# Two residual additions of a four-layer graph network made by accumulating DMAs instead of VectorE

## The chip, the cores and the metric

The kernel runs on one core of a Trainium2 chip. The core has TensorE (PE, matrix products), VectorE (DVE), ScalarE (ACT), GpSimd (POOL) and SyncE (SP, which here only issues DMAs), each with an instruction queue of its own that is worked off in order, and 16 DMA engines that all queues share. The metric is the device time of one execution in microseconds; less is better.

## The reference

32 batches of 512 tokens with 128 features pass through four residual layers, all with one 512x512 adjacency matrix. Cut to what matters (`ln_relu` is the normalization of a token's features followed by max with 0):

```python
# layer 0: graph convolution
h = ln_relu(x);  x = x + (A_norm @ h) @ W.T + b0        # A_norm: normalized adj + I
# layer 1: five gated steps
h0 = h = ln_relu(x)
for _ in range(5):
    m = adj @ h                                          # used for both m_in and m_out
    u3 = h @ u3_w.T + u3_b
    z = sigmoid([m, m] @ w3_w.T + w3_b + u3)
    r = sigmoid([m, m] @ w4_w.T + w4_b + u3)
    hv = tanh([m, m] @ w5_w.T + w5_b + (r * h) @ u5_w.T + u5_b)
    h = (1 - z) * h + z * hv
x = x + h
# layers 2 and 3: attention over the edges of adj
x = x + elu(attention(ln_relu(x)));  x = x + attention(ln_relu(x))
```

The two additions that the change touches are the `+ b0` of layer 0 and the `x + h` at the end of layer 1.

## The kernel before, in words

Everything stays in fp32 in SBUF. A batch's x is one tile of 128 partitions by 4 token chunks by 128 features (256 KB, 2 KB in each partition). There are nine such tiles, and later four more in the memory of the transposed adjacency, which the profile calls "adjT".

Each batch goes through these stages:

- `gcn` (layer 0), for pairs of batches: `norm_relu` takes statistics on VectorE (L508, L512), computes factor and offset with four small GpSimd operations (L520, L521, L522, L525), and normalizes on ScalarE (L527). `in_three` multiplies by the adjacency in three rounded products (L644), with a rescaling by ScalarE (L626) in between. `out_mm` multiplies by W (L717). L704 adds b0 to x, and L725 adds the product. For the first four batches (`first`) L721 does the last step chunk by chunk.
- `ggnn` (layer 1): five times `step`, in six lanes, so that six batches are under way at once. The products are L644, L755 and L758, the gates are ScalarE's L788, L795, L799, and VectorE's L790 to L804 form the new state `new`, which has features on the partitions.
- After a step `shuttle` turns the state back to tokens on the partitions: VectorE transposes blocks of 32 by 32 into `sq` (L594), four DMAs write these to the DRAM tile `far` (L597), and one DMA reads it back into `h` (L599). After the last step L819 adds `h` to x. Steps that lie very early or late in the order go through TensorE instead (L586), and L812 adds; for the last step these are batches 28 to 31. `shuttle_first` (L604, L607, L610) does the same way back in the other direction before the first step.
- `gat` for layers 2 and 3: statistics and normalization as above, products L871, scores L914, mixing L940 (or L926 for the last batches), and the residual additions L955 to L973.

No loop issues these instructions directly. Every stage is handed as an `op` to a planner (`Plan`), with an engine, an assumed duration, a due time, the values it reads and writes, and a delay until its result is to be used. The planner simulates the engines in 16 attempts, chooses the attempt with the earliest end, and emits the instructions in that order. So each engine's order is fixed at build time, and durations and delays in the source decide it. Its prices on the lines concerned are 0.6 us for a large VectorE operation, 0.44 and 0.4 us for an SP issue, 1.2 us for each small GpSimd operation of a norm, and 4 and 5 us for a DMA's landing. An `op` with an empty function only marks an order. A `lane` is held by a batch from its first step to its last addition into x.

Of the kernel before, what the change touches and what calls it, by code (L numbers as in the profile page):

```python
# [14 lines left out]
ALU = mybir.AluOpType  # L15

P = 128
# [4 lines left out]
Q = P // W  # L22
# [248 lines left out]
def gnn_stack(ctx: ExitStack, tc: tile.TileContext, a: dict, out: bass.AP):  # L271
    nc = tc.nc
    x, adj = a["x"], a["adj"]
    B, N, D = x.shape
    C = N // P
# [9 lines left out]
    def flat(t):  # L285
        return t.rearrange("p c k -> p (c k)")
# [35 lines left out]
    op = plan.op  # L322
    MM, MM1, TURN, MR = 0.858, 0.224, 0.111, 0.2325
    V, A, COPY = 0.6, 0.575, 0.505
# [12 lines left out]
    def load(name, shape, src, due, kind=None, delay=4.7):  # L337
        v = Val(kind) if kind else fixed(shape, name)
        op("SP", 0.45, due, lambda: nc.sync.dma_start(matrix(v)[:, :shape[1]], src), w=[v], delay=delay)
        return v  # L340
# [20 lines left out]
    xs = []  # L361
# [6 lines left out]
    for c in range(C):  # L368
        e, q = (("ACT", nc.scalar), ("SP", nc.sync))[c % 2]
        op(e, 0.45, -1001, lambda c=c, q=q: q.dma_start(adj_sb.t[:, c, :], adj[c * P:(c + 1) * P, :]),  # L370
           w=[adj_sb[c]], delay=(3.2, 4.7, 4.4, 4.9)[c])
    w0 = load("w0", [P, D], a["L0_gnn_W"], -993.9, "m", delay=5.6)
    b0 = load("b0", [P, D], bass.AP(tensor=a["L0_gnn_b"].tensor, offset=a["L0_gnn_b"].offset,
                                    ap=[[0, P], [1, D]]), -993.4)

    op("DVE", 0.2, -38.7, lambda: nc.vector.tensor_scalar_add(b0.t, b0.t, -1.0), w=[b0])
    for k in ("w4", "w3", "w5", "u3", "u5"):
        src = a[f"L1_gnn_{k}_w"]
# [17 lines left out]
    for c in range(C):  # L396
        p = Val("bank")
# [16 lines left out]
    for m in range(C):  # L414
        op("DVE", 0.26, -800 + 0.7 * m, lambda m=m: nc.vector.tensor_add(diag.t[:, m, :], block(adjT.t, m), ident.t),
           r=[adjT, ident], w=[diag[m]])
# [69 lines left out]
    for k, u, half in (("w4", "u3", True), ("w3", "u3", True), ("w5", "u5", False)):  # L486
        gate_b[k] = fixed([P, 1], "gate_b" + k)
        op("DVE", 0.1, -14, lambda k=k, u=u: nc.vector.tensor_add(gate_b[k].t, raw["b" + k].t, raw["b" + u].t),
           r=[raw["b" + k], raw["b" + u]], w=[gate_b[k]])
# [4 lines left out]
    for i, l in enumerate((2, 3)):  # L494
        p = Val("bank")
        op("PE", 0.3, 9, lambda i=i, l=l, p=p: nc.tensor.matmul(p.t[:, 0, :2], gats.t[:, i, :], a_pair[l].t, start=True, stop=True),
           r=[gats, a_pair[l]], w=[p])
# [89 lines left out]
        op("PE", C * TURN, due, turns, r=[y, ident], w=[p, *then])  # L587
        return p

    def shuttle(src, squares, dst, due, soon):  # L590


        sq, far = Val("sq"), Val("far", Q)
        op("DVE", 0.626, soon, lambda: nc.vector.transpose(  # L594
            sq.t.rearrange("p q (c j) -> p q c j", c=C), flat(src.t).rearrange(squares, c=C, q=Q)), r=[src], w=[sq])
        for k in range(Q):
            op("SP", 0.44, due, lambda k=k: nc.sync.dma_start(  # L597
                far.t[:, :, k, :].rearrange("q i f -> i q f"), sq.t[k * W:(k + 1) * W]), r=[sq], w=[far[k]], delay=4)
        op("SP", 0.4, due, lambda: nc.sync.dma_start(dst.t, far.t.rearrange("q i k f -> (q i) k f")), r=[far], w=[dst], delay=5)  # L599

    def shuttle_first(h, hT, due, soon):
# [94 lines left out]
    def gcn(pair, due):  # L696
        first, ys = pair[0] < 4, []
        for i, b in enumerate(pair):
            y = Val("y", C)
            if b == 0:  # L700
                norm_first(b, y)
            else:
                norm_relu(b, y, -797 if b == 1 else due + i, dinv if first else None)
            op("DVE", V, due + i + 3.8, lambda b=b: nc.vector.tensor_add(  # L704
                xs[b].t, xs[b].t, b0.t[:, None, :].to_broadcast([P, C, D])), r=[b0], w=[xs[b]])
            ys.append(y)

        ms = [product(y, due + i) if first else in_three(y, False, factors["an"], due + i) for i, y in enumerate(ys)]
        if b == 1:
            factors["adj"] = factors_of(adjT, "adj", -3.6, ys[0])  # L710
            factors["an"] = normalized(ms[0])
        for i, (b, m) in enumerate(zip(pair, ms)):
            p = Val("bank")

            def out_mm(m=m, p=p):
                for c in range(C):
                    nc.tensor.matmul(p.t[:, c, :], m.t[:, c, :], w0T.t[:, 0, :], start=True, stop=True)  # L717
            op("PE", C * MM1, due + i + 3.3, out_mm, r=[m, w0T], w=[p])
            if first:
                for c in range(C):  # L720
                    op("DVE", 0.26, due + i - 0.5, lambda b=b, c=c, p=p: nc.vector.scalar_tensor_tensor(  # L721
                        xs[b].t[:, c, :], p.t[:, c, :], dinv.t[:, c:c + 1], xs[b].t[:, c, :], op0=ALU.mult, op1=ALU.add),
                       r=[p, dinv], w=[xs[b][c]])
            else:
                op("DVE", V, due + i + 1.5, lambda b=b, p=p: nc.vector.tensor_add(flat(xs[b].t), flat(xs[b].t), flat(p.t)),  # L725
                   r=[p], w=[xs[b]])
# [23 lines left out]
    def step(b, s, m, hT, due, lane):  # L750
        gate, r, rh, z, cand = Val("bank"), Val("r"), Val("rh"), Val("z"), Val("bank")
        split = isinstance(m, tuple)

        def weigh(p, i, moving, start=False, of=None):
            nc.tensor.matmul(flat(p.t), (of or gates).t[:, i, :], flat(moving.t), start=start, stop=True, skip_group_check=True)  # L755

        def one_pass(p, i, moving, start, of):
            nc.tensor.matmul(flat(p.t), of.t[:, i - 1, :], flat(moving.t), start=start, stop=True, skip_group_check=True)  # L758

        def by_m(p, i, at, start, *more):  # L760

            rest = [x for _, _, reads in more for x in reads]

            def others():
                for of, moving, _ in more:
                    weigh(p, 0, moving, of=of)
            if not split:
                def whole():
                    weigh(p, i, m, start)
                    others()  # L770
                op("PE", (1 + len(more)) * MM, at, whole, r=[m, gates, *rest], w=[p])
                return
            upper, lower, across = m
            upper_of, lower_of, across_of = of_gates

            def first_two():
                one_pass(p, i, upper, start, upper_of)
                one_pass(p, i, lower, False, lower_of)

            def third_one():  # L780
                one_pass(p, i, across, False, across_of)
                others()
            op("PE", 2 * MR, at, first_two, r=[upper, lower, upper_of, lower_of], w=[p])
            rescale(p, at - 5)
            op("PE", MR + len(more) * MM, at, third_one, r=[across, across_of, *rest], w=[p])

        by_m(gate, 1, due + 0.2, True, (gates, hT, [hT, gates]))
        op("ACT", A, due - 5, lambda: nc.scalar.activation(flat(r.t), flat(gate.t), AF.Tanh, bias=gate_b["w4"].t, scale=0.5),  # L788
           r=[gate, gate_b["w4"]], w=[r])
        op("DVE", V, due - 5, lambda: nc.vector.scalar_tensor_tensor(flat(rh.t), flat(r.t), 1.0, flat(hT.t), op0=ALU.add, op1=ALU.mult),  # L790
           r=[r, hT], w=[rh])
        if split:
            rescale(gate, due - 5, 1 / (1 + 1 / SPLIT))
        by_m(gate, 2, due + 0.3, False)
        op("ACT", A, due - 5, lambda: nc.scalar.activation(flat(z.t), flat(gate.t), AF.Tanh, bias=gate_b["w3"].t, scale=0.5),  # L795
           r=[gate, gate_b["w3"]], w=[z])
        hv, new = Val("hv"), Val("hT")
        by_m(cand, 3, due + 0.4, True, (u5T, rh, [rh, u5T]))
        op("ACT", A, due - 5, lambda: nc.scalar.activation(flat(hv.t), flat(cand.t), AF.Tanh, bias=gate_b["w5"].t),  # L799
           r=[cand, z, gate_b["w5"]], w=[hv])  # L800
        op("DVE", V, due - 5, lambda: nc.vector.tensor_sub(flat(hv.t), flat(hv.t), flat(hT.t)), r=[hT], w=[hv])  # L801
        op("DVE", V, due - 5, lambda: nc.vector.scalar_tensor_tensor(flat(hv.t), flat(z.t), 1.0, flat(hv.t), op0=ALU.add, op1=ALU.mult),
           r=[z], w=[hv])
        op("DVE", V, due - 5, lambda: nc.vector.scalar_tensor_tensor(flat(new.t), flat(hv.t), 0.5, flat(hT.t), op0=ALU.mult, op1=ALU.add),  # L804
           r=[hv, hT], w=[new])

        last = s == STEPS - 1
        h = Val("h", C)
        if not EARLY <= due < STEPS * B:
            p = to_features(new, due + 2, *([] if last else [h]))  # L810
            if last:
                op("DVE", V, due + 2, lambda: nc.vector.tensor_add(flat(xs[b].t), flat(xs[b].t), flat(p.t)),  # L812
                   r=[p, lane], w=[xs[b]])
            else:
                op("ACT", COPY, due + 1, lambda: nc.scalar.copy(flat(h.t), flat(p.t)), r=[p], w=[h])
            return h, False, new
        shuttle(new, "p (c q i) -> p q c i", h, due, due - 5)
        if last:
            op("DVE", V, due + 2, lambda: nc.vector.tensor_add(  # L819
                xs[b].t.rearrange("p c (k j) -> p k c j", k=Q), xs[b].t.rearrange("p c (k j) -> p k c j", k=Q),  # L820
                h.t.rearrange("p k (c j) -> p k c j", c=C)), r=[h, lane], w=[xs[b]])
        return h, True, new


# [210 lines left out]
```

## Time and profile before

| | before |
|---|---|
| median of 3 runs | 1515.34 us (1513.87 to 1516.15) |
| profiled execution | 1513.58 us, span 1511.7 us |
| PE busy | 1498.9 us (99%) |
| PE weight load busy | 1153.8 us (76%) |
| DVE busy | 1430.9 us (95%), 3431 instructions |
| ACT busy | 1236.2 us (82%) |
| POOL busy | 292.9 us (19%), 496 instructions |
| DMA of SP's queue | 155.66 MB, 39.6% of 16 engines' time |
| granted TensorE clock | 1.0 |

Busy time is the time in which at least one instruction of the engine is recorded. The records of VectorE's large operations overlap a little, so the spacing of their starts (0.60 us) is below a record's length (0.68 us). Ends of matmuls are modelled. The times of a row's instructions are means over one execution.

### The profile page before, as it was taken

To read this page: it belongs to the slowest core of one execution; us is meant where nothing else is said; L and a number is where in the kernel's file an instruction comes from. 1 tells how busy PE (TensorE), PEld (TensorE's weight loads), DVE (VectorE), ACT (ScalarE), POOL (GpSimd) and SP (SyncE) were. 2 spreads that over 40 slices of the span, in tenths; PEclk is the share of its full clock that TensorE was granted. 3 is DMA by queue.
4 is the path that set the end of the run, shared out by engine and by line. 5 is a ranking of instruction groups with operands and counts; after the bars stand their busy time and mean duration, and the time that the engine had idled before them with its cause. 6 is when DMAs were issued, how large, how long until landed. Compare 5 with 4: busy or idle time off the path is not lost.

```text
span 1511.7 us, 24916 instructions
## 1 busy us (share of the span) xinstructions
PE 1498.9 (99%) x7366; PEld 1153.8 (76%) x7366; DVE 1430.9 (95%) x3431; ACT 1236.2 (82%) x2720; POOL 292.9 (19%) x496
## 2 busy tenths in 40 slices
PE   8999999999999999999999999999999999999998
PEld 7666677777777777777787877877777787767788
DVE  8989989999999999999999999999999999898798
ACT  7966888888888888988889888798988978877764
POOL 5412010221221211220222121111221110111111
PEclk9999999999999999999999999999999999999999
DMA  4143333444434444444444453444434444342111
GB/s 112 36 95 108 84 90 106 116 122 119 112 102 116 126 120 127 124 112 105 124 120 101 113 133 105 113 119 120 126 91 127 120 104 118 86 132 71 36 41 44
DMA packets 270151, 157.77 MB, mean 104 GB/s; under 512 B 81248, under 2 KB 236224, under 8 KB 270016
## 3 DMA queue, kind: packets, MB, share of 16 engines
q1 hardware_dynamic: 269728, 155.66, 39.6%
q8 instruction: 58, 0.95, 0.3%
q14 instruction: 77, 0.63, 0.1%
q10 hardware_dynamic: 288, 0.52, 0.1%
HBM read 86.25 MB, written 69.84 MB: 103 GB/s over the span
## 4 chain that ended last, share of the span: by engine, by line
PE 95%; DVE 3%; ACT 1%; DMA 1%; issue 0%; ACTq 0%
PE bank L644 34%; PE bank L755 21%; PE bank L758 19%; PE bank L940 13%; PE bank L871 4%; PE bank L717 2%; PE bank L926 1%; PE bank L586 1%; DVE e L914 1%; DMA rh<-in_L_gnn_w_w_dram 0%; DMA e<-in_adj_dram 0%; PE bank L667 0%; DVE x L721 0%; DVE st L563 0%; DVE e L685 0%
## 5 line engine op out<-in xcount | busy, mean ns | idle before, releaser
L626 ACT ACTIVATE bank<-bank 128x512 f32<-128x512 f32 x748 | 426.6, 595 | 103.3 <-PE bank L644 72.8
L520 POOL TENSOR_TENSOR rstd<-mv,eps 128x4 f32<-128x4 f32 x119 | 59.2, 497 | 1110.2 <-DVE mv L512 1049.1
L940 PEld LDWEIGHTS bank<-h_gat,e 128*128 128x128 f32 x1792 | 218.1, 191 | 24.2 <-issue 17.0
L620 DVE SCALAR_TENSOR_TENSOR across<-lower,upper 128x512 fp32r<-128x512 f32 x328 | 219.7, 676 | 4.2 <-PE bank L758 2.4
L940 PE MATMUL bank<-h_gat,e 128*128 128x129 f32 x1792 | 220.3, 275 | 0.0
L758 PE MATMUL bank<-upper,gates 128*128 128x512 f32 x420 | 205.2, 489 | 0.0
L758 PE MATMUL bank<-across,gates 128*128 128x512 f32 x420 | 198.8, 487 | 0.2 <-ACT bank L626 0.2
L644 PE MATMUL bank<-adj,upper 128*128 128x512 f32 x640 | 189.6, 418 | 0.7 <-ACT upper L617 0.7
L644 PE MATMUL bank<-adj,across 128*128 128x512 f32 x640 | 189.8, 419 | 0.0
L644 PE MATMUL bank<-adj,lower 128*128 128x512 f32 x640 | 175.4, 396 | 0.0
L758 PE MATMUL bank<-lower,gates 128*128 128x512 f32 x420 | 165.5, 394 | 0.0
L755 PE MATMUL bank<-hT,wT 128*128 128x512 f32 x320 | 163.3, 592 | 0.0
L755 PE MATMUL bank<-rh,wT 128*128 128x512 f32 x320 | 163.3, 592 | 0.0
L914 DVE SCALAR_TENSOR_TENSOR e<-row,h_gat,maskT 128x512 f32<-128x512 f32 x224 | 156.8, 741 | 0.0
L644 PEld LDWEIGHTS bank<-adj,across 128*128 128x128 f32 x640 | 118.3, 188 | 42.4 <-issue 16.5
L644 PEld LDWEIGHTS bank<-adj,upper 128*128 128x128 f32 x640 | 118.3, 188 | 41.1 <-issue 14.4
L644 PEld LDWEIGHTS bank<-adj,lower 128*128 128x128 f32 x640 | 120.5, 188 | 28.6 <-DVE lower L618 0.4
L788 ACT ACTIVATE r<-bank,gate_bw 128x512 f32<-128x512 f32 x160 | 111.7, 698 | 36.8 <-PE bank L755 34.6
L521 POOL TENSOR_TENSOR rstd<-rstd,mhalf 128x4 f32<-128x4 f32 x119 | 135.6, 1140 | 0.0
L801 DVE TENSOR_TENSOR hv<-hv,hT 128x512 f32<-128x512 f32 x160 | 108.7, 680 | 19.1 <-ACT hv L799 18.3
L795 ACT ACTIVATE z<-bank,gate_bw 128x512 f32<-128x512 f32 x160 | 110.4, 692 | 18.1 <-PE bank L758 15.4
L799 ACT ACTIVATE hv<-bank,gate_bw 128x512 f32<-128x512 f32 x160 | 111.2, 696 | 11.9 <-PE bank L755 11.7
(162 smaller groups left out, 2843.3 us busy)
## 6 DMA issues: line engine op xcount, KB each, us to landing
far<-sq SPq DMA_DIRECT2D x928, 64.0 KB
h<-far SPq DMA_DIRECT2D x148, 256.0 KB
gT<-far SPq DMA_DIRECT2D x56, 256.0 KB
row<-line SPq DMA_DIRECT2D x56, 256.0 KB
hT<-far SPq DMA_DIRECT2D x112, 64.0 KB
x<-in_x_dram SPq DMA_DIRECT2D x24, 256.0 KB
out_dram<-x SPq DMA_DIRECT2D x20, 256.0 KB
adjT<-in_x_dram SPq DMA_DIRECT2D x8, 256.0 KB
```

The lines of the kernel that those rows point to most:

```text
L521: op("POOL", 1.2, due, lambda: nc.gpsimd.tensor_tensor(rstd.t, rstd.t, mhalf.t, ALU.pow), r=[mhalf], w=[rstd])
L620: op("DVE", V, due - 5, lambda: nc.vector.scalar_tensor_tensor(flat(across.t), flat(lower.t).bitcast(F32), -SPLIT, flat(upper.t).bitcast(F ...
L626: op("ACT", COPY, due, lambda: nc.scalar.mul(flat(p.t), flat(p.t), by), w=[p])
L644: nc.tensor.matmul(flat(p.t), left.t[:, c, :], right.t[:, c, :], start=first and c == 0, stop=c == C - 1, skip_group_check=True)
L755: nc.tensor.matmul(flat(p.t), (of or gates).t[:, i, :], flat(moving.t), start=start, stop=True, skip_group_check=True)
L758: nc.tensor.matmul(flat(p.t), of.t[:, i - 1, :], flat(moving.t), start=start, stop=True, skip_group_check=True)
L788: op("ACT", A, due - 5, lambda: nc.scalar.activation(flat(r.t), flat(gate.t), AF.Tanh, bias=gate_b["w4"].t, scale=0.5), r=[gate, gate_b["w ...
L795: op("ACT", A, due - 5, lambda: nc.scalar.activation(flat(z.t), flat(gate.t), AF.Tanh, bias=gate_b["w3"].t, scale=0.5), r=[gate, gate_b["w ...
L799: op("ACT", A, due - 5, lambda: nc.scalar.activation(flat(hv.t), flat(cand.t), AF.Tanh, bias=gate_b["w5"].t), r=[cand, z, gate_b["w5"]], w ...
L801: op("DVE", V, due - 5, lambda: nc.vector.tensor_sub(flat(hv.t), flat(hv.t), flat(hT.t)), r=[hT], w=[hv])
L914: op("DVE", 0.661, due + 3, lambda j=j: nc.vector.scalar_tensor_tensor(e.t[:, j, :], matrix(row), h.t[:, j, D + 1:D + 2], mask.t[:, j, :], ...
L940: nc.tensor.matmul(pt()[:, c, :D + 1], e.t[:, j, i * P:(i + 1) * P], h.t[:, j, :D + 1], start=(j == 0), stop=(j == C - 1))
```

## The change

In `gcn`, for all but the first four batches, VectorE's addition of b0 becomes a DMA issued by GpSimd whose source is b0 repeated over the four chunks, and which adds into x. In `shuttle`, after the last step, the DMA that reads `far` back into `h` and the VectorE addition that follows become four DMAs issued by GpSimd, one for each block of 32 features, which read `far` and add into x. Each of the four waits for all of `far` and for the lane; an empty `op` marks the moment at which all four have landed. The planner is given 1.1 us for each such issue, and 3.5 and 5 us until it has landed. Nothing else is changed in the source, but the planner makes the whole order anew.

```diff
-    def shuttle(src, squares, dst, due, soon):
+    def shuttle(src, squares, dst, due, soon, onto=None):
...
         for k in range(Q):
             op("SP", 0.44, due, lambda k=k: nc.sync.dma_start(
                 far.t[:, :, k, :].rearrange("q i f -> i q f"), sq.t[k * W:(k + 1) * W]), r=[sq], w=[far[k]], delay=4)
+        if onto:
+            x, lane = onto
+            for k in range(Q):
+                op("POOL", 1.1, due, lambda k=k: nc.gpsimd.dma_start(
+                    x.t.rearrange("p c (k j) -> p k c j", k=Q)[:, k],
+                    far.t.rearrange("q i k (c j) -> (q i) k c j", c=C)[:, k], accum_op=ALU.add),
+                   r=[far, lane], w=[x[k]], delay=5)
+            op("SP", 0.0, due, lambda: None, w=[x], delay=0)
+            return
         op("SP", 0.4, due, lambda: nc.sync.dma_start(dst.t, far.t.rearrange("q i k f -> (q i) k f")), r=[far], w=[dst], delay=5)
...
-            op("DVE", V, due + i + 3.8, lambda b=b: nc.vector.tensor_add(
-                xs[b].t, xs[b].t, b0.t[:, None, :].to_broadcast([P, C, D])), r=[b0], w=[xs[b]])
+            if first:
+                op("DVE", V, due + i + 3.8, lambda b=b: nc.vector.tensor_add(
+                    xs[b].t, xs[b].t, b0.t[:, None, :].to_broadcast([P, C, D])), r=[b0], w=[xs[b]])
+            else:
+                op("POOL", 1.1, due + i + 3.8, lambda b=b: nc.gpsimd.dma_start(
+                    xs[b].t, b0.t[:, None, :].to_broadcast([P, C, D]), accum_op=ALU.add), r=[b0], w=[xs[b]], delay=3.5)
...
-        shuttle(new, "p (c q i) -> p q c i", h, due, due - 5)
-        if last:
-            op("DVE", V, due + 2, lambda: nc.vector.tensor_add(
-                xs[b].t.rearrange("p c (k j) -> p k c j", k=Q), xs[b].t.rearrange("p c (k j) -> p k c j", k=Q),
-                h.t.rearrange("p k (c j) -> p k c j", c=C)), r=[h, lane], w=[xs[b]])
+        shuttle(new, "p (c q i) -> p q c i", h, due, due - 5, (xs[b], lane) if last else None)
         return h, True, new
```

## The prediction

> **What bounds the kernel now.** I read three views in this order: busy time by stretch, the chain of waits, and the groups of the engines that the change touches.
>
> The first view is the busy time of each engine in stretches of 100 us (columns: stretch, its length, then busy us and instruction count of PE, PEld, DVE, ACT, POOL, granted clock, DMA share, GB/s).
>
> ```profile
> 0.00:100.00 100.00, 94.24 (x427) 68.87 (x428) 88.61 (x272) 79.34 (x167) 40.13 (x68) 1.00 0.33 81
> 500.00:600.00 100.00, 100.00 (x508) 78.52 (x507) 99.66 (x233) 86.61 (x195) 17.51 (x32) 1.00 0.48 125
> 1100.00:1200.00 100.00, 98.75 (x480) 76.44 (x479) 97.79 (x232) 83.36 (x186) 21.20 (x36) 1.00 0.44 115
> 1400.00:1500.00 100.00, 98.10 (x665) 82.59 (x664) 89.84 (x279) 63.29 (x181) 15.18 (x16) 1.00 0.13 37
> 1500.00:1511.00 11.00, 7.84 (x71) 7.64 (x69) 8.11 (x28) 1.92 (x8) 0.00 (x0) 0.97 0.27 79
> ```
>
> TensorE is idle for 5.8 us in the first 100 us, for 1.25 us once between 1100 and 1200, and for 1.9 + 3.2 us from 1400 on. Each stretch between that is not shown has 100.00. VectorE is nearly as full in places (99.66 of 100), so one could take it for the bound.
>
> A busy TensorE need not be a fast one, so I price its work from the second view, the chain that ended last (start, us, what):
>
> ```profile
> PE 95%; DVE 3%; ACT 1%; DMA 1%; issue 0%; ACTq 0%
> ...
> 128.36 3.43 PE bank L755 x8
> ...
> 545.47 3.57 PE bank L940 x32
> ...
> 1106.76 5.59 PE bank L644 x24
> ```
>
> Uninterrupted pieces give 5.59 / 24 = 0.233 us for a 512-column matmul on the rounded operands, 3.43 / 8 = 0.429 for a plain one, 3.57 / 32 = 0.112 for a 129-column one. With the counts of the groups: L644 2256 x 0.233 = 525; L758 1260 x 0.233 = 293; L755 760 x 0.429 = 326; L940, L926, L871 and L717 2816 x 0.112 = 315; the remaining 274 small ones some 35. That is about 1494 of 1511.7 us. So TensorE works at its own rate almost everywhere: an edit off TensorE can win only the 1.25 us in the middle and part of the 5.1 us at the end (the 5.8 us at the start lie before the first changed instruction matters).
>
> The third view is the groups concerned (busy us, mean ns, idle before and its releaser):
>
> ```profile
> L704 DVE TENSOR_TENSOR x<-x,b 128x512 f32<-128x512 f32 x24 | 16.0, 674 | 0.7 <-ACT y L527 0.7
> L819 DVE TENSOR_TENSOR x<-x,h 128x512 f32<-128x512 f32 x20 | 13.6, 681 | 0.0
> L704 DVE TENSOR_TENSOR adjT<-adjT,b 128x512 f32<-128x512 f32 x8 | 5.5, 683 | 0.1
> L819 DVE TENSOR_TENSOR adjT<-adjT,h 128x512 f32<-128x512 f32 x8 | 5.4, 669 | 0.0
> L521 POOL TENSOR_TENSOR rstd<-rstd,mhalf 128x4 f32<-128x4 f32 x119 | 135.6, 1140 | 0.0
> ```
>
> "adjT" is the same x in the four buffers that the transposed adjacency gives back. Nobody waits for these additions beyond tenths of a microsecond. The list of waits says the same from the other side: TensorE never waits for GpSimd, and ScalarE does so once for 0.4 us. The waits are the other way round:
>
> ```profile
> POOL rstd L520 <- DVE mv L512: 1049.1, 98, 37.9
> ```
>
> GpSimd is busy for 292.9 us and spends most of the remainder waiting for VectorE's statistics.
>
> **What the Trainium skill says.** "Perfetto Trace Analysis", Identifying the Most-Contended Engine, warns that matmul occupancy does not tell the distance to the limit; hence the pricing above, which here agrees with the 99%. "SBUF — State Buffer", Who interferes with whom, says that a VectorE instruction with two SBUF inputs contends with a GpSimd instruction that reads SBUF. The trace agrees: the same 128x4 addition of L520 takes 0.20 us in some records and 0.55 in others. The page expects no such quarrel for an instruction that only writes, and infers that descriptor generation needs the write side; no instruction of the kernel before tests it. "DMA: Bandwidth & Descriptors", Issuing engines are not separate DMA queues: transfers of all issuers share 16 DMA engines. The queue table shows SP's queue taking 39.6% of them.
>
> **Part 1: x + b0, batches 4 to 31.** Removed: of the 24 + 8 = 32 VectorE additions the 28 that don't belong to the first four batches. Their records last 0.68 us, but in the timeline two such instructions start 0.60 apart, so 28 x 0.60 = 16.8 us of VectorE. Added: 28 GpSimd DMAs of 256 KB in 512-byte runs. Such an addition must follow ScalarE's four L527 reads of x and come before L725. Paired in order, L725 starts 5 to 215 us after L704, 53 us in the median, so a landing of several us is hidden by the way through `in_three` and `out_mm`.
>
> **Part 2: x + h, batches 0 to 27.** Removed: 28 additions, again 16.8 us of VectorE, and 28 h<-far issues (0.338 us median in the records of `far`), 9.5 us of SP and a wait for `far` on SP's queue. Added: 4 x 28 = 112 GpSimd DMAs of 64 KB, each in 512 runs of 128 bytes, and an empty order mark. The wait for `far` moves to GpSimd's queue; behind it stand the next L520 to L525 groups, for which ScalarE's L527 wait. In the SP list, L599 waits for far<-sq at most 2.9 us, against 4 us in the plan, so by the planned time `far` has normally landed.
>
> **Price of a GpSimd DMA.** There is no row for it. From below I take SP's issue, 0.43; the plan writes 1.1; from above I allow 3 us, since 512 runs are many and nothing here shows the generator's speed. The landing priced by the skill (same DMA page, Anatomy of one DMA, 2.0 us + bytes / 436 GB/s) is an estimate of 2.2 us for 64 KB and 2.6 for 256 KB, without accumulation; the plan has 5 and 3.5. I take 1.1 us, because the plan's other prices lie on the trace (0.60 against 0.60 spacing on VectorE, 0.44 against 0.433 on SP, 0.2325 against 0.233 on TensorE). GpSimd then gets 140 x 1.1 = 154 us more: 293 + 154 = 447, 30% of the span. It has a cushion: the plan prices the four operations of a norm at 4 x 1.2 = 4.8 us, while the rows give 0.50 + 1.14 + 0.39 + 0.44 = 2.5. Pairing the 119 L525 records with the 119 groups of L527 in order, ScalarE takes up a norm 14 us after it is ready in the median; in one of four pairs it is under 7.7, in one of ten under 3.2.
>
> **DMA engines.** A packet of 128 bytes takes 13 ns in the trace, one of 512 bytes 27, one of 2 KB 84. Part 2 removes 28 x 128 x 84 / 16 = 19 us for each DMA engine and adds 28 x 2048 x 13 / 16 = 47; part 1 adds 28 x 512 x 27 / 16 = 24. Net +52 us, 3.4% of the span; with each accumulating packet at double price +8%. From 40% that is no bound.
>
> **Sum.** VectorE loses 33.6 us of work, but TensorE can take back at most 1.25 us plus a part of 5.1. The last lines of the end belong to batches 28 to 31, whose x + h stays on VectorE, so I take 0 there. Since the planner makes a whole new order from the new prices, small differences of either sign come with it; the trace bounds them below by those same idle times, and above I allow 3 us. What is late next if an addition's cover goes: VectorE's L508 of the following normalization, which in the trace starts 0.5 us after L819 and now has to stand for the landing; the plan puts other work there. Gain 0 to 1, cost of new waits 0 to 3: zero. The profiled execution took 1513.58 us and the median of the runs is 1515.34; I carry zero on to the median's scale and say 1515.
>
> **The rivals.** Differences under 0.2% (3 us) can't be told from no change here.
>
> *VectorE stands for x that lands late (slower).* Place: the first L508 after x + h. If an issue costs c, the fourth of the burst goes out 4 x (c - 1.1) later than planned, and VectorE, in order, stands. It has won 33.6 / 28 = 1.2 us for each batch, and its idle time from 100 to 1400 us is 55.6 us by the stretches, 2.0 for each batch. From a lateness of 3.2 us (c = 1.9) VectorE is the bound; at c = 2 it costs 28 x (3.6 - 3.2) = 11 us, so 1526; at c = 2.5, 67 us, so 1582. For it: VectorE's 99.66 of 100, and the unseen 512 runs. Against: the plan's price. Chance 0.37.
>
> *The four accumulations wait for one another (slower, and in a sense another change than the one described).* If the writes into interleaved columns of one x were ordered, three landings of about 2.2 us stand in GpSimd's queue: 28 x (6.6 - 3.2) = 95, so 1610. Against: L610 writes hT in the same interleaved columns, and its four issues follow each other at 0.5 us without a wait. Chance 0.05.
>
> *VectorE is the bound already (faster).* Then 33.6 us would come back: 1482. Against: TensorE's 1494 us of work exclude it. A gain is capped by 1.25 + 5.1, which gives 1509 to 1512 if the new order happens to close those gaps. Chance 0.08.
>
> **How the numbers follow.** No change 0.50, slower 0.37 + 0.05 = 0.42, faster 0.08. The likeliest case alone reaches from 1512 to 1518. The range goes down to 1511, into the faster case, and up to 1534, which takes in c slightly above 2 and leaves out some 0.13 above and 0.05 below.
>
> **What would show it.** Right: TensorE at 100.00 in the middle stretches, VectorE some 34 us less busy, GpSimd's DMA issues about 1.1 us apart, no L508 wait on a DMA. Wrong: issues 2 us or more apart, VectorE or ScalarE idle before L508 or L527 for a DMA or GpSimd, PE below 99 in the stretches from 100 to 1400.

## The result, and the profile after

The changed kernel takes 1520.19 us in the median of 6 runs (1519.78 to 1523.46), the kernel before 1514.61 us beside it (1513.65 to 1516.15): a ratio of 1.0039 with the interval [1.0026, 1.0051], 5.6 us slower. The forecast was no change, at 1515. The profiled execution of after took 1520.31 us, its span 1518.5 us.

The busy times and the DMA queues from the page of after:

```profile
PE 1504.8 (99%) x7376; PEld 1153.0 (76%) x7376; DVE 1403.5 (92%) x3375; ACT 1233.7 (81%) x2720; POOL 451.5 (30%) x636
...
q1 hardware_dynamic: 265696, 148.32, 38.8%
q0 software_dynamic: 73920, 14.69, 12.8%
...
x<-b POOLq DMA_DIRECT2D x20, 256.0 KB, 4.8
x<-far POOLq DMA_DIRECT2D x80, 64.0 KB, 4.9
```

The edit does what it says. VectorE has 56 instructions less and is busy for 27 us less, GpSimd has 140 more and is busy for 451.5 us, and the queue q0 (GpSimd's) appears. The last number of the two issue rows is the median time to landing in us. TensorE shows 10 more instructions: the planner puts transposes of nothing into pauses that it foresees late in the kernel, and in the new order it foresaw ten (they stand at 1500 to 1502 us, when most of the loss shown below has long arisen).

The groups of GpSimd's DMAs (busy us, mean ns of a record, idle before and its releaser):

```profile
L602 POOL DMA_DIRECT2D x<-far x80 | 106.4, 2148 | 44.9 <-DMA far<-sq 43.5 <-issue 1.3
L602 POOL DMA_DIRECT2D adjT<-far x32 | 42.4, 2032 | 15.4 <-DMA far<-sq 14.6 <-issue 0.8
L717 POOL DMA_DIRECT2D x<-b x20 | 26.7, 1362 | 125.9 <-ACT y L527 109.0 <-ACT bank L635 13.2 <-DMA hT<-far 3.7
L717 POOL DMA_DIRECT2D adjT<-b x8 | 10.5, 1311 | 28.3 <-ACT y L527 27.4 <-PE bank L768 0.9
```

The records of L602 overlap, so the price of an issue is busy time over count: (106.4 + 42.4) / 112 = 1.33 us, and (26.7 + 10.5) / 28 = 1.33 us for L717. The page "Perfetto Trace Analysis" of the Trainium skill, GPSIMD Engine Instruction, advises to time GpSimd by the spacing of the starts of consecutive instructions and not by reported durations. The durations would indeed mislead (2.1 us in the mean), but so would the starts here: where one of the 112 DMAs stands directly behind another, the starts lie 0.75 us apart in the median and the ends 1.31. The ends are what holds GpSimd, for a small operation that starts within the record of a DMA ends only after that DMA, in all 27 cases of after.

The stretches of after (columns as before; the first line is the one of before between 300 and 400, for comparison):

```profile
300.00:400.00 100.00, 100.00 (x488) 78.09 (x487) 97.48 (x232) 86.64 (x190) 21.45 (x36) 1.00 0.44 116
...
0.00:100.00 100.00, 93.24 (x421) 67.78 (x422) 81.41 (x261) 77.52 (x162) 38.58 (x73) 1.00 0.44 92
300.00:400.00 100.00, 98.68 (x483) 76.30 (x482) 95.83 (x230) 85.49 (x192) 32.00 (x47) 1.00 0.58 119
500.00:600.00 100.00, 100.00 (x507) 78.34 (x506) 96.09 (x229) 86.59 (x194) 31.07 (x46) 1.00 0.55 113
```

VectorE, 99.66 before between 500 and 600, is down to 96.09, and TensorE isn't faster for it. Between 300 and 400 TensorE has 1.3 us of idle time that it did not have. But its idle time in the whole span is only 13.7 us against 12.8: most of the loss lies in gaps that the modelled ends of the matmul records cover. So I compared the traces by work: each matmul priced at its uninterrupted spacing, and the times taken at which both kernels had done the same amount. After is behind before by 2.4 us when 30 us of TensorE's work are done, 5.0 us at 400, 6.3 at 640 and 7.0 at 1000; its last matmul ends 7.3 us later than before's (1515.1 against 1507.8 us of the span).

The chain of after around its one large stop (start, us, what):

```profile
355.43 0.69 ACT r L801
356.12 0.58 ACT z L808
356.69 0.49 ACT bank L635
357.18 0.60 ACT hv L812
357.78 0.24 ACT h L527
...
359.41 1.56 ACT y L527 x4
360.97 0.49 ACT bank L635
361.46 0.04 issue
361.50 0.50 PE bank L771
```

TensorE waits for ScalarE's rescaling L635, which the order has put behind four L527 of another batch. No DMA and no GpSimd instruction is in this chain. Nor does any instruction of after stand for an accumulated x: the list of waits has none on `x<-far`, `x<-b` or the same in `adjT`.

### The profile page after: what moved, and what is told of

It is laid out like the page before. It is cut to its first block, busy times and chain, and to the rows that moved or that the text cites. A ratio compares the mean times of both kernels' runs of the same rounds, so it can differ in the third digit from the quotient of the medians.

```text
span 1518.5 us, 25301 instructions
## 1 busy us (share of the span) xinstructions
PE 1504.8 (99%) x7376; PEld 1153.0 (76%) x7376; DVE 1403.5 (92%) x3375; ACT 1233.7 (81%) x2720; POOL 451.5 (30%) x636
## 3 DMA queue, kind: packets, MB, share of 16 engines
q1 hardware_dynamic: 265696, 148.32, 38.8%
q0 software_dynamic: 73920, 14.69, 12.8%
## 4 chain that ended last, share of the span: by engine, by line
PE 91%; DVE 5%; ACT 2%; DMA 1%; issue 0%; SPq 0%; ACTq 0%; DVEq 0%
PE bank L653 33%; PE bank L768 21%; PE bank L771 18%; PE bank L949 13%; PE bank L880 3%; PE bank L730 2%; PE bank L935 1%; DVE e L923 1%; ACT bank L635 1%; PE bank L586 1%; PE bank L676 0%; DMA e<-in_adj_dram 0%; DVE lower L627 0%; DVE across L629 0%; DMA rh<-in_L_gnn_w_w_dram 0%
## 5 line engine op out<-in xcount | busy, mean ns | idle before, releaser
L635 ACT ACTIVATE bank<-bank 128x512 f32<-128x512 f32 x748 | 424.4, 594 | 101.2 <-PE bank L653 68.3
L520 POOL TENSOR_TENSOR rstd<-mv,eps 128x4 f32<-128x4 f32 x119 | 54.4, 457 | 770.5 <-DVE mv L512 729.3
L629 DVE SCALAR_TENSOR_TENSOR across<-lower,upper 128x512 fp32r<-128x512 f32 x328 | 219.3, 677 | 5.8 <-PE bank L771 2.9
L771 PE MATMUL bank<-across,gates 128*128 128x512 f32 x420 | 206.0, 503 | 1.3 <-ACT bank L635 1.3
L771 PE MATMUL bank<-upper,gates 128*128 128x512 f32 x420 | 198.0, 471 | 0.0
L521 POOL TENSOR_TENSOR rstd<-rstd,mhalf 128x4 f32<-128x4 f32 x119 | 152.8, 1285 | 0.0
L803 DVE SCALAR_TENSOR_TENSOR rh<-r,hT 128x512 f32<-128x512 f32 x160 | 109.0, 681 | 18.4 <-ACT r L801 18.0
```

The costliest lines, as they stand in the source:

```text
L521: op("POOL", 1.2, due, lambda: nc.gpsimd.tensor_tensor(rstd.t, rstd.t, mhalf.t, ALU.pow), r=[mhalf], w=[rstd])
L635: op("ACT", COPY, due, lambda: nc.scalar.mul(flat(p.t), flat(p.t), by), w=[p])
```

## The experiments

Two theories. **"DMAs"**: the transfers cost the time, by their issue on GpSimd, their landing or their load on the DMA engines. **"Order"**: the planner, given other prices, made another order, and this order is the loss, whatever is issued in it.

### Order and instructions exchanged

**The old order with the DMAs** (`e1_old_order_dma`): the planner gets the operations of before; only what they emit is changed.

```diff
-            op("DVE", V, due + i + 3.8, lambda b=b: nc.vector.tensor_add(...), r=[b0], w=[xs[b]])
+            op("DVE", V, due + i + 3.8, add_b0, r=[b0], w=[xs[b]])     # the DMA for b >= 4
...
-        op("SP", 0.4, due, lambda: nc.sync.dma_start(dst.t, far...), r=[far], w=[dst], delay=5)
+        op("SP", 0.4, due, back, r=[far], w=[dst], delay=5)            # last step: the four DMAs
...
-            op("DVE", V, due + 2, lambda: nc.vector.tensor_add(...), r=[h, lane], w=[xs[b]])
+            op("DVE", V, due + 2, lambda: None, r=[h, lane], w=[xs[b]])
```

Expected:

> The instructions of the kernel after, in the order of the kernel before: the planner is given the old operations and prices, and only what they emit is exchanged (the b0 addition emits the accumulating DMA, the read-back of far emits the four accumulating DMAs, the later addition emits nothing). Theory 'order' (the loss comes from the new order that the planner makes, the DMAs themselves are hidden): no change from before, 1514 to 1517. Theory 'DMAs' (issue, landing and waits of the DMAs cost what was lost): 1519 to 1522, since the same DMAs run, and here without any time planned for them on GpSimd, so rather more than after.

Measured: 1526.36 us (5 runs), before 1515.21; ratio 1.0075 [1.0062, 1.0087]. So in an order that has no place for them the DMAs do cost, 11 us, which "order" had not expected. The list of waits of this run tells which engines stood for them (engine and line, waited for, us in total, times, longest):

```profile
ACT y L527 <- POOL off L525: 12.1, 6, 3.1
...
DVE st L508 <- DMA x<-far: 6.6, 5, 3.5
...
DVE st L508 <- DMA adjT<-far: 3.0, 2, 2.6
```

Both waits that the prediction named as signs of being wrong are here. Such a wait costs time only where it reaches TensorE; the timeline shows one place where it does (start, us, instruction, idle before):

```profile
1173.69 5.27 POOL L604 DMA_DIRECT2D adjT<-far  x4
...
1177.35 2.99 POOL L521 TENSOR_TENSOR rstd<-rstd,mhalf 128x4 f32<-128x4 f32 x1
...
1180.42 0.20 POOL L525 TENSOR_TENSOR off<-off,rstd 128x4 f32<-128x4 f32 x1
...
1180.66 1.65 ACT L527 ACTIVATE y<-x,off,rstd 128x128 f32<-128x128 f32 x4 [3.08 <-POOL off L525]
...
1182.82 0.69 DVE L626 TENSOR_TENSOR lower<-bank,upper 128x512 fp32r<-128x512 f32 x1 [3.09 <-ACT upper L625]
1183.32 0.50 PE L770 MATMUL bank<-across,gates 128*128 128x512 f32 x1 [1.70 <-ACT bank L634]
```

Read downwards: four issues hold GpSimd for 5.3 us, to 1178.96; L521, a small operation of a norm, has its start recorded before that but ends only at 1180.34; ScalarE stands 3.1 us for the offset that follows, VectorE 3.1 us for ScalarE, and TensorE 1.7 us.

**The new order with the additions** (`e2_new_order_dve`): the planner gets the operations of after, but VectorE adds.

```diff
-                    xs[b].t, b0..., accum_op=ALU.add), r=[b0], w=[xs[b]], delay=3.5)        # nc.gpsimd.dma_start
+                    xs[b].t, xs[b].t, b0...), r=[b0], w=[xs[b]], delay=3.5)                 # nc.vector.tensor_add
...
-                op("POOL", 1.1, due, <DMA k>, r=[far, lane], w=[x[k]], delay=5)
-            op("SP", 0.0, due, lambda: None, w=[x], delay=0)
+                op("POOL", 1.1, due, <SP reads far into h at k = 0>, r=[far, lane], w=[x[k], dst[k]], delay=5)
+            op("SP", 0.0, due, <VectorE adds h to x>, r=[dst], w=[x], delay=0)
```

Expected:

> The instructions of the kernel before, in the order of the kernel after: the planner is given the new operations and prices, but where the first of the four DMAs would be issued SP reads far back into an h buffer, at the moment where all four should have landed VectorE adds, and the b0 addition is VectorE's in the place of its DMA. Theory 'order': 1518 to 1522, like after. Theory 'DMAs': 1513 to 1516, like before.

Measured: 1527.66 us (4 runs); ratio to before 1.0084 [1.007, 1.0098], 7.5 us above after. An order that has no place for the additions does not take them either. The exchange shows that each set of instructions wants the order planned for it; it does not yet split the 5.6 us.

### The order alone

**After's order with nothing in it** (`a_none`), and **before's order with nothing in it** (`b_none`). In both the functions of the changed `op`s are empty, so the order stays, and the additions go out of the computation. The edit shown is `a_none`'s; in `b_none` the 56 VectorE additions are emptied in the same way, and SP's read-back of `far` stays.

```diff
-                op("POOL", 1.1, due, lambda k=k: nc.gpsimd.dma_start(...), r=[far, lane], w=[x[k]], delay=5)
+                op("POOL", 1.1, due, lambda: None, r=[far, lane], w=[x[k]], delay=5)
...
-                op("POOL", 1.1, due + i + 3.8, lambda b=b: nc.gpsimd.dma_start(...), r=[b0], w=[xs[b]], delay=3.5)
+                op("POOL", 1.1, due + i + 3.8, lambda: None, r=[b0], w=[xs[b]], delay=3.5)
```

Expected:

> The order of the kernel after with nothing in the place of the changed additions: neither the DMAs nor VectorE additions are emitted (x + b0 of batches 4 to 31 and x + h of batches 0 to 27 are left out of the computation). What is left is the new order alone. Theory 'order' (within the order planned for them the DMAs are hidden; the order is the loss): 1518 to 1521, like after. Theory 'DMAs': 1512 to 1516, since no DMA of GpSimd is left.

> The order of the kernel before with the same additions left out, VectorE's 56 (x + b0 of batches 4 to 31, x + h of batches 0 to 27); the read-back of far into h stays. Both theories: 1512 to 1516, so VectorE's 34 us are worth nothing in the order that had a place for them. A result under 1510 would say that VectorE was a bound after all. Against the 1526 of the same order with the DMAs it also gives what unplanned DMAs cost.

Measured: `a_none` 1521.41 us (5 runs), before 1515.74, ratio 1.0040 [1.0028, 1.0052]. With no DMA of GpSimd left the loss is complete. `b_none` 1514.07 us (13 runs), ratio 0.9992 [0.9984, 1.0000]: without its 56 additions VectorE gives back at most a microsecond or two.

The chain of `a_none` at the place shown of after:

```profile
356.46 0.69 ACT r L798
357.15 0.58 ACT z L805
357.74 0.49 ACT bank L633
358.22 0.60 ACT hv L809
...
360.45 1.57 ACT y L527 x4
362.02 0.49 ACT bank L633
362.51 0.04 issue
362.56 0.50 PE bank L768
```

It is the same stop, 1.0 us later, with the same links (lines are shifted by 3 or 2). The comparison by work gives the same picture over the whole span: `a_none` is behind before by 3.5, 6.1, 7.3 and 8.0 us at the four points where after is behind by 2.4, 5.0, 6.3 and 7.0, and its last matmul ends 8.2 us later than before's, where after's ends 7.3 later. The two differ by 0.9 to 1.1 us everywhere, a difference that is there from the first 30 us on, while the first DMA of GpSimd in after is issued at 56 us. From the point at 30 us to the last matmul after loses 4.9 us and `a_none` 4.7. So in after the DMAs cost nothing that this comparison can see.

The difference at the start has a reason of its own, the clock. Between 10 and 30 us the granted clock (third number from the end) was 1.00 in the profiled execution of after and 0.91 in that of `a_none`:

```profile
10.00:30.00 20.00, 17.59 (x117) 15.04 (x117) 18.04 (x74) 13.03 (x30) 9.20 (x18) 1.00 0.37 95
...
10.00:30.00 20.00, 18.21 (x108) 15.61 (x108) 16.20 (x62) 11.46 (x26) 9.97 (x15) 0.91 0.34 86
```

The trace of `a_none` records one stretch of 3.4 us at half clock there, which is worth 1.7 us by estimate. `b_none` has the same stretch (0.91) and lags behind before by 2.1 us from the first 10 us of work on, and by nothing more up to the end.

### Other orders of the same instructions

**One price of before** (`b_price`), **one price of both** (`b_628`, `a_628`), and **the issue prices of after** (`a_measured`):

```diff
 b_price
-            op("DVE", V, due + i + 3.8, lambda b=b: nc.vector.tensor_add(       # V = 0.6
+            op("DVE", 0.59, due + i + 3.8, lambda b=b: nc.vector.tensor_add(
 b_628 and a_628, in shuttle and shuttle_first
-        op("DVE", 0.626, soon, lambda: nc.vector.transpose(
+        op("DVE", 0.628, soon, lambda: nc.vector.transpose(
 a_measured
-                op("POOL", 1.1, due, lambda k=k: nc.gpsimd.dma_start(
+                op("POOL", 2.0, due, lambda k=k: nc.gpsimd.dma_start(
-                op("POOL", 1.1, due + i + 3.8, lambda b=b: nc.gpsimd.dma_start(
+                op("POOL", 1.3, due + i + 3.8, lambda b=b: nc.gpsimd.dma_start(
```

Expected:

> The kernel before with one number changed: the planner's price of the b0 addition 0.59 us in place of 0.60. Same instructions on every engine, another order. Theory 'order': the planner's result scatters by several us for next to no reason, so this may lie anywhere from 1512 to 1523, and I expect 1518 to 1523. Theory 'DMAs': 1513 to 1517, no change from before.

> The kernel before with the planner's price of VectorE's block transposes 0.628 us in place of 0.626, same instructions, another order. Theory 'order': between 1512 and 1523, a draw; the middle of the draws is above 1515, so I expect 1516 to 1520. Theory 'DMAs': 1513 to 1517.

> The kernel after with the same nudge, 0.628 in place of 0.626, same instructions as after, another order. Theory 'order': a draw between 1512 and 1524; I expect 1514 to 1518, so that the pair with the same nudge is turned round, the DMAs not slower than the additions. Theory 'DMAs': 1519 to 1523, above its partner without DMAs by 4 us or more.

> The kernel after with two prices changed to what the profile of after shows: 1.3 us for a b0 issue and 2.0 us for each of the four others, in place of 1.1. Same instructions on every engine, another order. Theory 'order': another draw, 1513 to 1518, I expect 1515 to 1517. Theory 'DMAs' in its form 'the issues are longer than planned': an improvement on after by the time that engines stood for late landings; in its form 'the DMAs cost whatever the order': 1519 to 1522.

Measured, each with before beside it:

| kernel | additions by | us (runs) | ratio to before |
|---|---|---|---|
| `b_price` | VectorE | 1521.57 (5) | 1.0045 [1.0032, 1.0058] |
| `b_628` | VectorE | 1520.23 (6) | 1.0031 [1.0020, 1.0043] |
| `a_628` | DMAs | 1515.41 (22) | 1.0002 [0.9996, 1.0009] |
| `a_measured` | DMAs | 1517.63 (21) | 1.0017 [1.0010, 1.0023] |

A hundredth of a microsecond in one planned price loses at least as much as the change did. The instructions are the same but for TensorE's transposes of nothing, of which `b_price` has 19 and `b_628` 16, all after 1459 us. The same nudge of 0.002 us makes before slower by 4.5 us and leaves the kernel with the DMAs where before was. The price of 2.0 us in `a_measured` came from the records' mean; the 1.33 us were read only afterwards.

In `b_price` a stop looks different. Its chain between 355 and 380 us:

```profile
369.34 0.41 ACT upper L617
369.75 5.51 DMA h<-far
375.26 0.02 issue
375.28 0.63 ACT upper L617
...
376.45 3.06 PE bank L644 x12
```

Here ScalarE stands for the last 2.6 us of a read-back of `far` (by the list of waits), an SP transfer that both kernels have. So the places at which an order loses are not the same from order to order.

### Chosen orders

**The best of 40 orders with DMAs** (`a_best`) and **of 40 with additions** (`b_best`), each chosen by the planner's own estimate of its end, with the price of VectorE's block transposes varied:

```diff
 a_best: a_measured, and
-        op("DVE", 0.626, soon, lambda: nc.vector.transpose(
+        op("DVE", 0.634, soon, lambda: nc.vector.transpose(
 b_best: before, and
-        op("DVE", 0.626, soon, lambda: nc.vector.transpose(
+        op("DVE", 0.622, soon, lambda: nc.vector.transpose(
```

Expected:

> The kernel after with prices of 1.3 and 2.0 us for the DMA issues and 0.634 in place of 0.626 for VectorE's block transposes: of 40 such orders the one whose planned end was the earliest. Same instructions as after. Theory 'order': 1511 to 1515, at least as fast as before, so that the loss of after isn't bound to its DMAs. Theory 'DMAs': not below 1518.

> The kernel before with 0.622 in place of 0.626, chosen in the same way from 40 orders. Same instructions as before. Theory 'order': 1511 to 1515, within 3 us of the best order with DMAs. Theory 'DMAs': 1511 to 1515, at least 4 us below the best order with DMAs.

Measured: `a_best` 1511.47 us (13 runs), ratio 0.9978 [0.9970, 0.9986]; `b_best` 1512.94 us (13 runs), ratio 0.9987 [0.9979, 0.9996]. The version with DMAs beats before and after, and it issues the same 140 DMAs as after:

```profile
300.00:400.00 100.00, 100.00 (x474) 76.65 (x473) 95.53 (x229) 87.89 (x195) 29.65 (x47) 1.00 0.56 122
```

These are its stretch from 300 to 400 us: TensorE without a pause, GpSimd and the DMA engines about as busy as in after. Part of the distances is the granted clock: counting only the executions with a mean granted clock of 1.0, `a_best` takes 1511.45 us (12 of 13), `b_best` 1512.65 (7 of 13) and before beside them 1513.96 (7 of 25). That the remaining lead of 1.2 us over `b_best` comes from the DMAs isn't shown; orders of either kind differ by more.

## Why the prediction was wrong, and where it was right

**What bounds the kernel** was right. `b_none` takes VectorE's 34 us away and wins next to nothing. VectorE at 99.66 was no second bound.

**The step that failed is in the sum**: "small differences of either sign come with it", bounded below by TensorE's idle times and above by 3 us. The planned orders of one and the same set of instructions lie between 1512.94 and 1521.57 us with the additions and between 1511.47 and 1520.19 us with the DMAs, 9 us each. That term, carried into the sum as zero, was the whole effect of the change, 5.6 us: after's order without any of the changed instructions has the loss (1.0040 against 1.0039). The bound of 3 us had no reason in the profile. The measured 1520.19 lies inside the stated range only because that range was opened upwards for another reason, the late landing, which did not come. Before's order was one draw, and it left TensorE almost without a gap, so a new one had little to win and much to lose: of the five other orders that were not chosen by their planned end (after, `b_price`, `b_628`, `a_628`, `a_measured`), four are slower than before and none is faster. The idle times that I used as the limit of a gain were the hint, and I didn't read them as a limit on one side only.

**The rivals.** The late landing on which VectorE stands was given the chance of a slower result. Its mechanism exists, as `e1_old_order_dma` shows, but it isn't what slowed after, where L508 never waits for an accumulated x. The issue price from which this rival decides, 1.9 us, is not reached at 1.33. Above all the landings are in time: the plan has 4 x 1.1 + 5 = 9.4 us from the first issue of a batch to the last landing, and the 26 such groups that after's trace shows unbroken took 8.4 us in the median, 10.2 at most. Waits between the four accumulations do not appear either: four landings of 4.9 us one after another would take 19.6. Of the prediction's signs of being wrong only one showed in after, TensorE at 98.68 between 300 and 400 us, and the chain there leads to ScalarE's place in the order, not to a DMA.

**The prices.** An issue is 1.33 us by the rows, not 1.1, and GpSimd's 451.5 us against my 447 came out nearly right by luck: in `a_none`, with the same order and no DMAs, GpSimd is busy for 278.9 us where I took 293, and the 140 issues add 173 where I took 154. The landing is 4.8 to 5.1 us in the medians of after's four groups. My estimate from "DMA: Bandwidth & Descriptors" (Anatomy of one DMA) was 2.2 and 2.6, without accumulation; the measurement decides. The plan's 5 for x + h fits, and its 3.5 for b0 is too short. The DMA engines' load was undersized: I had 3.4 to 8% more, and it is 38.8 + 12.8 - 39.6 = 12%. In the trace of after a packet of 128 bytes of GpSimd's queue takes 36 ns in the median (13 in SP's), one of 512 bytes 68 ns (27 in SP's). The comparison with `a_none` shows no cost of this load.

**The start.** 2.4 us of after's lag arise in the first 30 us, before any DMA of GpSimd and with the granted clock at 1.00 in both profiled executions. `a_none` lags by 3.5 there, about 1.8 without the estimated 1.7 us of its half-clock stretch. So a good part of it comes with the order; how much is chance of one execution isn't shown.

**What stays open**: whether orders with the DMAs are on the average better or worse than orders with the additions. Unselected ones gave 1520.2, 1517.6 and 1515.4 us against 1515, 1521.6 and 1520.2; that is too few to say. Nor is the loss of after followed gap by gap: the stop shown holds TensorE for a part of it only, and why the planner makes better or worse orders from nearly equal prices was not looked into.

## What to carry to other kernels

Where a planner makes the order, an edit is two changes: other instructions, and another draw of the order. Measure the draw by itself, by nudging a price that changes no instruction, before a difference of its size is put down to the edit; and split an edit by emitting nothing in the new order's slots. A kernel whose bound engine has hardly a gap is a good draw, and the next one is likelier to lose than to win.

## What the runs showed of the hardware

- A GpSimd DMA of 512 runs that accumulates into SBUF holds GpSimd for 1.33 us in after, with runs of 128 and of 512 bytes alike. The recorded starts of such DMAs follow each other faster (0.75 us) than their ends (1.31 us). The DMA lands 4.5 to 5.2 us after its issue, by the medians of the groups of after and `a_best`.
- Its packets take 2.5 to 2.8 times as long on the DMA engines as SP's plain ones of the same size (36 against 13 ns, 68 against 27 ns, medians of after). Whether this is the accumulation or the issuing queue isn't separated.
- VectorE is hardly slowed while GpSimd issues DMAs: in after the two-input instruction L629 takes 681 ns in the mean of the 44 records that lie wholly within a GpSimd DMA record, and 677 in the 187 with nothing of GpSimd beside them. The page "SBUF — State Buffer", Who interferes with whom, expects a VectorE instruction with two SBUF inputs to contend with a GpSimd instruction that reads SBUF, not with one that only writes it, and infers that descriptor generation needs the write side; this trace agrees.
- The granted clock of TensorE can differ between executions of one order in the first 30 us: `b_none` and `a_none` have one record of 3.4 us at half clock from about 11 us on, before and after have none there. Of before's 25 executions beside `a_best`, the 7 with a mean clock of 1.0 took 1513.96 us in the median and the other 18, at 0.997 to 0.999, 1515.89. What sets it off isn't shown.
